# Cross attention and a soft mixture of experts: both halves of a second product planned as one step

## The chip, the cores and the metric

The kernel runs on one core of a Trainium2 chip. The metric is the time of one execution on the device in microseconds (us); the median of several executions is compared. The engines of the core work at the same time, each through its own instructions in the order in which the program lists them: TensorE (PE, with its weight loads PEld) multiplies matrices into PSUM, VectorE (DVE), ScalarE (ACT) and GpSimd (POOL) do elementwise work, and SyncE (SP) starts transfers.

## The reference

Inputs are x (16 batches of 100 tokens, 256 features) and a context (16 x 361 x 256). All numbers are float32.

```python
x = x + xattn(layernorm(x), ctx)          # 16 heads of 16, softmax over 361 keys
z = layernorm(x)
n = layernorm(z) * norm_g + norm_b
logits   = n @ slots_embedded.T           # 100 tokens x 16 experts x 64 slots
dispatch = softmax(logits, axis=tokens)
combine  = softmax(logits, axis=all 1024 slots)
slots = dispatch.T @ n                    # for each expert 64 slots of each batch
h     = gelu(slots @ Wg[e] + bg[e]) * (slots @ Wu[e] + bu[e])   # 256 -> 512
eout  = h @ Wd[e] + bd[e]                 # 512 -> 256
out   = x + combine @ eout
```

Each of the 16 experts has its own three weight matrices of 512 KB; every batch sends 64 slots through every expert.

## The kernel before

The 16 batches go through in five groups, `GROUPS = (2, 2, 4, 4, 4)`. For every group there is attention, then dispatch (logits, softmax over tokens, slots) in quarters of four experts and pairs of batches, then the 16 experts, then the combining of the experts' outputs. The weights of all experts are loaded anew for every group, through six buffers of 512 KB (`load_weights`, `give_back`).

**Products of an expert.** `experts(g)` takes one expert after the other. The first products are made in parts: a PSUM bank `gp` (gate) and a bank `up`, eight matmul instructions each in groups of four batches. ScalarE reads `gp` through gelu into `ge` (L1286), VectorE multiplies with `up` into `hT` (L1291). The second product, `down(g, e, hts)`, takes a pair of experts at once: the first one's 64 slots fill the upper half of the bank's partitions, the second one's the lower half. A bank `dn` holds two batches (2 x 256 columns), so a pair needs one bank in a group of two batches and two banks in a group of four. The loop over `half` makes these banks; each has 32 matmul instructions (L1235) and one VectorE addition of the bias (L1244), which writes `ring`. `down` is called behind the first part of the next pair's first expert (L1304), and once at the end of the group (L1312). After both halves the two experts' `Wd` buffers are given back and refilled.

**Who sets the order.** The program's order is written when the kernel is built, by a planner in the main loop (L1342 to L1465). Every stream of work is a generator. It yields a time from which its next step can run and the number of PSUM banks that it needs; the planner keeps a clock of its own (`Clock`, with planned durations for every engine and a queue of four `mm` banks), and `Task.ready` is the later of that time and of the moment at which the first so many banks of the queue are free (L126, `bank_ready`). At each turn the planner takes the first task in its list that is ready, else the one that is ready soonest, and runs the generator up to its next yield; what lies between two yields stands in the program without a break. The list has attention's units, the dispatch tasks and the side work (keys, queries, output projections) ahead, and the experts last: experts fill whatever the others leave. Once the slots of the next expert are missing, experts aren't ready at all.

**The other streams that matter here.** A unit of attention (`units`, one batch and a quarter of the heads) has three pieces on TensorE: `maxima` (L781) with the `values` (L829) of the unit before, a small transposition in `queries` (L795), and the scores in `exponentials` (L806). Each waits for VectorE or ScalarE behind the one before it. All units share four PSUM banks of their own. `dispatch_quarter` makes logits (`lg`, L938), four exponentials, a reciprocal and a GpSimd product, and then the transposed weights `disp`. From the fourth group on VectorE makes these with 16 transpositions, two for each yield (L1004 to L1011); such a yield needs no bank and waits only until the planner's VectorE is less than 2.5 us behind (L1400 to L1402). Then come two slot products `sl` (L1028), evicted by VectorE and ScalarE. At most two dispatch tasks are in the planner's list at a time.

The four `mm` banks serve `gp`, `up`, `dn`, `cx`, `lg`, `sl`, `po` and the small tiles in turn. On the chip a matmul waits for the bank's last reader by semaphore, whatever the planner assumed.

Of the kernel before, what the change touches and what calls it, by code (L numbers as in the profile page):

```python
# [129 lines left out]
def xattn_ffn_kernel(  # L130
# [38 lines left out]
    def mm_tile(name):  # L169
        return ps_mm.tile([P, 512], F32, tag="mm", name=name)  # L170
# [743 lines left out]
    def eouts_of(g, q):  # L914
        return regions[g, q].rearrange("p (e b d) -> p e b d", e=QE // 2, d=D)
# [301 lines left out]
    def give_back(*names):  # L1217
        for n in names:
            w_free.append(slot_of[n])
            load_weights()  # L1220

    def down(g, e, hts):

        k = g * E + e
        q, j = divmod(e, QE)
        n = GROUPS[g]
        FB = 512 // (n * S)
        for half in range(n // 2):
            yield max(t for h in hts for _, t in h), 1
            dn = mm_tile("dn")  # L1230
            for i in range(2):
                b = 2 * half + i
                for fc in range(FC):
                    for x in range(2):
                        nc.tensor.matmul(  # L1235
                            dn[S * x : S * x + S, i * D : (i + 1) * D],
                            lhsT=hts[x][fc // FB][0].rearrange("p (f b s) -> p f b s", f=FB, s=S)[
                                :, fc % FB, b, :
                            ],
                            rhs=weights[k + x, "wd"][:, fc, :],  # L1240
                            start=fc == 0,
                            stop=fc == FC - 1,
                        )
            nc.vector.tensor_tensor(  # L1244
                eouts_of(g, q)[:, j // 2, 2 * half : 2 * half + 2, :],
                dn.rearrange("p (b d) -> p b d", d=D),
                biases[k // 2].unsqueeze(1).to_broadcast([P, 2, D]),
                ALU.add,
            )
            t = ck.psum_dve(512, ck.pe(2048, ck.bank()))  # L1250
            ck.free(t)
            done_t[g, q] = t
        give_back((k, "wd"), (k + 1, "wd"))

    def experts(g):
        n = GROUPS[g]
        T = n * S
        FB = 512 // T
        pair, to_combine = [], []
        for e in range(E):  # L1260
            k = g * E + e
            q, j = divmod(e, QE)
            hts = []
            for part in range(FC // FB):
                hT = const.tile([P, 512], F32, tag="hT", name="hT", bufs=5)
                ge = two.tile([P, 512], F32, tag="ge", name="ge")
                fcs = range(part * FB, (part + 1) * FB)
                for kind in range(2):
# [33 lines left out]
                if part == 0:  # L1302
                    if e % 2 == 0 and pair:
                        yield from down(g, e - 2, pair)  # L1304
                        pair = []
                    if e % QE == 1 and e > 1:
                        to_combine.append(q - 1)
                    while to_combine and all((g, p) in sums for p in range(n // 2)):
                        yield from combine_quarter(g, to_combine.pop(0))
            give_back((k, "wg"), (k, "wu"))  # L1310
            pair.append(hts)
        yield from down(g, E - 2, pair)  # L1312
        for q in to_combine + [NQ - 1]:
            yield from combine_quarter(g, q)
# [203 lines left out]
```

## Time and profile before

| | us |
|---|---|
| median of 3 runs | 1179.04 (1178.51 to 1179.66) |
| profiled execution | 1181.03 |
| its span, first to last instruction | 1179.2 |
| TensorE busy | 1160.4 |
| VectorE busy | 633.4 |
| ScalarE busy | 540.3 |
| GpSimd busy | 151.4 |
| first gp of the five groups | 84.2, 244.3, 441.6, 775.2, 984.0 |

The mean granted TensorE clock was 0.999. In the second products' row the page has 2048 matmul instructions (L1235), 232.9 us busy in all; every float32 product is two instructions. 512 of them belong to the two groups of two batches together, and 512 to each group of four. TensorE's matmuls overlap, so the duration of one (382 ns) is longer than the time from its start to the next; the time that a run of them holds the engine is read from start to start. The attention of the last group lies within the experts of the third and ends at 783 us; after that the order has experts, dispatch and combining alone.

### The profile page before, as it was taken

What the parts mean: (1) busy time and instruction counts of PE and PEld (TensorE: products, weight loads), DVE (VectorE), ACT (ScalarE), POOL (GpSimd) and SP (SyncE); (2) the same over time, 40 slices, a digit from 0 to 9 for tenths busy, and PEclk for the clock granted to TensorE, in tenths of its full rate; (3) what the DMA queues carried; (4) which work ended last, traced back from release to release, by engine and by line L of the source; (5) the groups of instructions that cost most, each with busy time, mean ns of one, the idle gap of its engine ahead of it and who ended that gap; (6) DMA issues with size and microseconds to landing.
All of it is one profiled execution on the core that took longest, in us unless ns stands there. A gap on an engine that the chain in (4) does not pass through costs nothing.

```text
span 1179.2 us, 24287 instructions
## 1 busy us (share of the span) xinstructions
PE 1160.4 (98%) x9815; PEld 898.6 (76%) x9815; DVE 633.4 (54%) x1559; ACT 540.3 (46%) x1112; POOL 151.4 (13%) x255
## 2 busy tenths in 40 slices
PE   8899999999999999999999999999999999999998
PEld 6588788787788877767777776787878878777876
DVE  5755445566654566655386767656543455432222
ACT  3547553565544667434454634646312336314110
POOL 3110301013000131300010010304000003002000
PEclk9999999999999999999999999999999999999999
DMA  4412666553466603223341321333344343344441
GB/s 133 133 33 83 233 195 202 163 140 120 130 221 224 188 11 90 83 53 106 112 106 54 110 90 39 98 126 112 112 159 138 115 148 126 112 132 159 140 129 55
DMA packets 138578, 144.85 MB, mean 123 GB/s; under 512 B 45040, under 2 KB 97218, under 8 KB 138466
## 3 DMA queue, kind: packets, MB, share of 16 engines
q1 hardware_dynamic: 137358, 141.60, 39.7%
q8 instruction: 78, 1.28, 0.4%
q0 software_dynamic: 496, 1.12, 0.3%
q10 hardware_dynamic: 612, 0.57, 0.2%
q14 instruction: 34, 0.28, 0.1%
HBM read 141.60 MB, written 1.66 MB: 121 GB/s over the span
## 4 chain that ended last, share of the span: by engine, by line
PE 95%; DVE 2%; ACT 2%; issue 1%; DMA 0%; POOL 0%; SPq 0%; ACTq 0%; DVEq 0%; POOLq 0%
PE dn L1235 19%; PE gp L1275 19%; PE up L1275 19%; PE sl L1028 5%; PE po L1157 5%; PE at L806 4%; PE at L781 4%; PE lg L938 3%; PE cx L829 3%; PE k_ps L609 3%; PE v_ps L669 3%; PE o_ps L722 1%; PE at L1329 1%; DVE mxp L786 1%; PE q_ps L538 1%; ACT d_ex L968 1%
## 5 line engine op out<-in xcount | busy, mean ns | idle before, releaser
L1275 PE MATMUL gp<-ring,w_all 128*128 128x256 f32 (+1 forms) x1280 | 247.8, 340 | 1.3 <-ACT lg_all L959 1.3
L1275 PE MATMUL up<-ring,w_all 128*128 128x256 f32 (+1 forms) x1280 | 246.6, 340 | 0.0
L1291 DVE SCALAR_TENSOR_TENSOR hT<-up,parT,ge 128x256 f32<-128x256 f32 (+1 forms) x320 | 119.7, 424 | 233.2 <-PE up L1275 164.3
L1235 PE MATMUL dn<-w_all,hT 128*64 128x256 f32 x2048 | 232.9, 382 | 0.1
L1286 ACT ACTIVATE ge<-gp,parT 128x256 f32<-128x256 f32 (+1 forms) x320 | 117.1, 430 | 249.3 <-PE gp L1275 245.2
L1275 PEld LDWEIGHTS gp<-ring,w_all 128*128 128x128 f32 x1280 | 203.4, 191 | 27.5 <-issue 4.9
L1275 PEld LDWEIGHTS up<-ring,w_all 128*128 128x128 f32 x1280 | 203.7, 191 | 21.4 <-issue 1.2
L1235 PEld LDWEIGHTS dn<-w_all,hT 128*64 128x64 f32 x2048 | 142.7, 137 | 78.5 <-issue 7.8
L786 DVE TENSOR_REDUCE mxp<-at 100x4 f32<-100x1444 f32 x64 | 106.3, 1661 | 30.9 <-PE at L781 30.2
L1244 DVE TENSOR_TENSOR ring<-dn,bd_bc 128x512 f32<-128x512 f32 x64 | 44.3, 692 | 134.8 <-PE dn L1235 133.2
L814 ACT ACTIVATE aT<-at 121x1200 f32<-121x1200 f32 x64 | 75.0, 1171 | 62.9 <-PE at L806 59.5
L1286 ACT ACT_TABLE_LOAD x60 | 77.0, 1283 | 26.7 <-PE gp L1275 26.0
L1008 DVE STREAM_TRANSPOSE disp<-d_ex 32x128 f32<-32x128 f32 x256 | 77.3, 302 | 4.5
L713 POOL TENSOR_TENSOR cxs<-cxs,rs 128x100 f32<-128x100 f32 x63 | 24.9, 398 | 389.3 <-DVE rs L710 361.9
L1043 ACT ACTIVATE ring<-sl,parT 128x256 f32<-128x256 f32 x64 | 32.7, 562 | 67.8 <-PE sl L1028 65.5
L1028 PE MATMUL sl<-disp,xn 100*128 100x256 f32 x256 | 63.4, 388 | 0.2 <-ACT disp L1021 0.2
L1157 PE MATMUL po<-ring,lg_all 128*100 128x256 f32 x256 | 60.5, 383 | 0.4 <-DVE ring L1244 0.2
L993 POOL TENSOR_TENSOR d_ex<-d_ex,d_sm 128x400 f32<-128x400 f32 x28 | 23.9, 854 | 267.6 <-DVE d_sm L990 240.6
L806 PEld LDWEIGHTS at<-q,kT 32*121 32x121 f32 x1344 | 40.6, 180 | 19.9 <-issue 8.8
L1028 PEld LDWEIGHTS sl<-disp,xn 100*128 100x128 f32 x256 | 46.4, 190 | 10.3 <-issue 2.6
L806 PE MATMUL at<-q,kT 32*121 32x100 f32 x1344 | 49.9, 277 | 3.4 <-DVE q L797 3.3
L814 ACT ACT_TABLE_LOAD x36 | 46.2, 1283 | 14.2 <-PE at L806 6.2
(152 smaller groups left out, 1268.8 us busy)
## 6 DMA issues: line engine op xcount, KB each, us to landing
w_all<-in_L_ffn_Wg_dram SPq DMA_DIRECT2D x80, 512.0 KB
w_all<-in_L_ffn_Wu_dram SPq DMA_DIRECT2D x80, 512.0 KB
w_all<-in_L_ffn_Wd_dram SPq DMA_DIRECT2D x80, 512.0 KB
bd_bc<-in_L_ffn_bd_dram SPq DMA_DIRECT2D x80, 64.0 KB
c_sb<-in_ctx_dram SPq DMA_DIRECT2D x96, 44.0 KB
out_dram<-acc SPq DMA_DIRECT2D x8, 200.0 KB
acc<-in_x_dram SPq DMA_DIRECT2D x7, 200.0 KB
ring<-n_L_ffn_slot_embeds_dram POOLq DMA_DIRECT2D x1, 1024.0 KB, 6.8
```

The lines of the kernel that those rows point to most:

```text
L781: nc.tensor.matmul(self.at[:N, r, :S2], lhsT=self.q[rows], rhs=self.k[rows], start=True, stop=True)
L786: nc.vector.tensor_reduce(mxv[:, :, m : m + 1], self.at[:N, :, :S2], AX.X, ALU.max, negate=True)
L806: nc.tensor.matmul(self.at[: KC + 1, r, c * N : (c + 1) * N], lhsT=self.k[rows, c * KC : c * KC + KC + 1], rhs=self.q2[rows], start=True, ...
L814: nc.scalar.activation(self.aT[: KC + 1], self.at[: KC + 1, :, : 3 * N], AF.Exp)
L1008: nc.vector.transpose(dst[toks, :, :, a, :], src[32 * a : 32 * a + 32, :, :, toks])
L1028: nc.tensor.matmul(sl[:, kd * 256 : (kd + 1) * 256], lhsT=xns[g][:, b0 + i, kd * P : (kd + 1) * P], rhs=disp[:, i, :], start=True, stop=True,)
L1157: nc.tensor.matmul(pos[i][:N, :D], lhsT=lg_all[:, slot, 2 * c + i, :], rhs=eouts_of(g, q)[:, c, 2 * p + i, :], start=c == 0, stop=c == 1,)
L1235: nc.tensor.matmul(dn[S * x : S * x + S, i * D : (i + 1) * D], lhsT=hts[x][fc // FB][0].rearrange("p (f b s) -> p f b s", f=FB, s=S)[:, fc ...
L1244: nc.vector.tensor_tensor(eouts_of(g, q)[:, j // 2, 2 * half : 2 * half + 2, :], dn.rearrange("p (b d) -> p b d", d=D), biases[k // 2].uns ...
L1275: nc.tensor.matmul(ps[:, f * T : (f + 1) * T], lhsT=w[:, kd, fc * P : (fc + 1) * P], rhs=slots_of(g, q)[:, j, kd].rearrange("p b s -> p (b ...
L1286: nc.scalar.activation(ge[:, cols], ps[:, cols], AF.Gelu, bias=col(8, e, fc))
L1291: nc.vector.scalar_tensor_tensor(out=hT[:, cols], in0=ps[:, cols], scalar=col(NPAR, e, fc), in1=ge[:, cols], op0=ALU.add, op1=ALU.mult,)
```

## The change

In `down` the yield moves out of the loop over the halves, and asks for as many banks as there are halves: one in groups of two batches, where the loop runs once, and two in groups of four. Both halves' matmuls and bias additions then follow each other in the program without a turn of the planner between them.

```diff
         n = GROUPS[g]
         FB = 512 // (n * S)
+        yield max(t for h in hts for _, t in h), n // 2
         for half in range(n // 2):
-            yield max(t for h in hts for _, t in h), 1
             dn = mm_tile("dn")
             for i in range(2):
                 b = 2 * half + i
```

## The prediction

> **What bounds the kernel now.** I read the page first (busy time, the chain that ended last), then the busy time by stage, then TensorE's waits from the point where the edit can act, and last the order of TensorE's and VectorE's work around single second products.
>
> ```profile
> PE 1160.4 (98%) x9815; PEld 898.6 (76%) x9815; DVE 633.4 (54%) x1559; ACT 540.3 (46%) x1112; POOL 151.4 (13%) x255
> PE 95%; DVE 2%; ACT 2%; issue 1%; DMA 0%; POOL 0%; SPq 0%; ACTq 0%; DVEq 0%; POOLq 0%
> ```
>
> The chain that ended last is 95% TensorE. By stage (columns: length, then busy time and count of PE, PEld, DVE, ACT, POOL, granted clock, DMA share, GB/s):
>
> ```profile
> 393.00:441.00 48.00, 45.66 (x329) 35.02 (x326) 31.03 (x73) 29.54 (x91) 16.21 (x21) 1.00 0.27 63
> 441.00:775.00 334.00, 333.02 (x3097) 244.36 (x3097) 213.04 (x502) 167.57 (x318) 43.44 (x68) 1.00 0.30 87
> 775.00:984.00 209.00, 208.91 (x1270) 166.31 (x1269) 101.95 (x275) 81.89 (x178) 18.60 (x29) 1.00 0.41 127
> 984.00:1180.00 196.00, 190.85 (x1133) 150.19 (x1131) 68.01 (x164) 51.77 (x101) 16.95 (x23) 1.00 0.40 124
> ```
>
> The first four-batch group's experts begin at 441 us, the next two groups' at 775 and 984. The edit can act from the first four-batch second product, at 470 us. TensorE idles 334.00 - 333.02 = 0.98 and 209.00 - 208.91 = 0.09 us in the first two stages; what is missing in the last is the tail after the last product (span end 1179.2). Its waits after 441 us are one:
>
> ```profile
> PE xn_t L748 <- ACT qp L551: 1.0, 1, 1.0
> ```
>
> So no second product waits for a bank. TensorE can end earlier only through 0.98 + 0.09 = 1.07 us of waits or through blocks that themselves become cheaper. That they can is seen in how a second product stands in the order. Split, then whole (start, length, line, tile, count):
>
> ```profile
> 554.86 3.67 PE L1235 MATMUL dn<-w_all,hT 128*64 128x256 f32 x32
> 558.47 0.89 PE L806 MATMUL at<-q,kT 32*121 32x100 f32 x24
> 559.29 3.67 PE L1235 MATMUL dn<-w_all,hT 128*64 128x256 f32 x32
> 562.89 0.87 PE L781 MATMUL at<-kT,qp 32*100 32x361 f32 x8
> ...
> 849.94 7.13 PE L1235 MATMUL dn<-w_all,hT 128*64 128x256 f32 x64
> 857.00 1.35 PE L1275 MATMUL gp<-ring,w_all 128*128 128x256 f32 x5
> ```
>
> A half alone holds TensorE 558.47 - 554.86 = 3.61 and 3.60 us, both halves in one run 857.00 - 849.94 = 7.06 us: 0.15 us less than 7.21.
>
> **The change part by part.** *The yields removed.* Three groups have four batches and eight pairs each, so 24 yields between two halves go. In groups of two batches n // 2 is 1, and nothing differs. Going through all 24 pairs in the trace, TensorE has other work between the halves in 11 (pairs 0 to 3 and 5 to 7 of the first such group, pairs 0 and 7 of the second, 2 and 3 of the last); 13 run whole already. Joining the 11 takes off 11 x 0.148 = 1.63 us, all on the path.
>
> *Where the displaced work goes.* Of the 11 insertions seven are attention's: maxima with values twice (pairs 0, 6), scores twice (2, 5), the small transposition of the maxima twice (1, 7), values with logits once (3). The other four are pieces of dispatch and combining. A displaced piece lands either at a border of gp or up with the joined product, or between gp and up. Start to start, gp and up hold TensorE 1.73 us between their like (785.67 to 787.40), 1.82 before maxima, scores, values or a second product (13 up blocks go straight into a second product, each at 1.82), and 1.83 after them or after a second product. At the border both surcharges are paid already, so the piece costs nothing new; between gp and up it costs 0.09 + 0.10 = 0.20 us. The transposition of the maxima costs 0.02 there, values with logits 0.09, the dispatch pieces nothing (gp beside sl, lg, po stays 1.73). If every displaced attention piece lands between gp and up: 4 x 0.20 + 2 x 0.02 + 0.09 = 0.93 us. Ends: 0, and 11 x 0.20 = 2.2 us. I take 0.93, because borders with second products are two for each pair and are mostly taken.
>
> *Two banks asked for.* The planner now calls the pair ready when the older two of four banks are free in its clock. The second of them belongs to a block at least two mm tiles back in the order, so some 3.5 us old where gp and up came last; only a modelled DVE or ACT queue longer than that delays it. Ends: 0, and one gp or up block (1.73 us) handed to other work in the wrong place now and then, which TensorE doesn't lose, since other work runs. I take 0. On the chip the matmuls still wait for their own banks alone.
>
> *Return of the weights.* give_back comes behind both halves as before; its loads on SP's queue move only with the order. No wait of TensorE on a weight stands in the list after 441 us, with the DMA engines at 0.30 to 0.41. I take 0; the cover is TensorE's own work.
>
> *Steps delayed behind the pair.* What could be planned between the halves now waits up to 3.5 us more. For attention this only exchanges the order of work while experts are there to fill. For dispatch it takes away a place for VectorE's transpositions, also in pairs that TensorE runs whole:
>
> ```profile
> 1027.81 0.88 DVE L1291 SCALAR_TENSOR_TENSOR hT<-up,parT,ge 128x256 f32<-128x256 f32 x2 [2.06 <-PE up L1275]
> 1028.71 0.62 DVE L1008 STREAM_TRANSPOSE disp<-d_ex 32x128 f32<-32x128 f32 x2
> 1031.35 0.69 DVE L1244 TENSOR_TENSOR ring<-dn,bd_bc 128x512 f32<-128x512 f32 x1 [2.02 <-PE dn L1235]
> 1032.07 0.61 DVE L1008 STREAM_TRANSPOSE disp<-d_ex 32x128 f32<-32x128 f32 x2
> 1034.83 0.69 DVE L1244 TENSOR_TENSOR ring<-dn,bd_bc 128x512 f32<-128x512 f32 x1 [2.14 <-PE dn L1235]
> ```
>
> Two transpositions follow each up block (every 3.45 us) and each half; a quarter has 16, so eight such steps. The step at 1032.07, planned between the halves, goes: 3.45 us for each pair that a quarter crosses. What that delays is the dispatch of the last group:
>
> ```profile
> 969.86 1.99 PE L1028 MATMUL sl<-disp,xn 100*128 100x256 f32 x8
> 971.69 1.52 PE L938 MATMUL lg<-xnT,seT 128*128 128x200 f32 x8
> 973.10 1.97 PE L1028 MATMUL sl<-disp,xn 100*128 100x256 f32 x8
> 974.90 1.52 PE L938 MATMUL lg<-xnT,seT 128*128 128x200 f32 x8
> 976.35 3.67 PE L1235 MATMUL dn<-w_all,hT 128*64 128x256 f32 x32
> ...
> 984.01 1.89 PE L1275 MATMUL gp<-ring,w_all 128*128 128x256 f32 x8
> ```
>
> The sl at 969.86 completes the last group's first quarter; its ScalarE eviction ends at 972.91, and the first gp that reads it starts at 984.01, so 11.1 us lie between. The quarter and the one queued before it cross four pairs from 890 to 976: at most 4 x 3.45 = 13.8 us later, some of it won back, because after a joined pair two steps follow within one gp block. Meanwhile TensorE still has the other sl and both lg of these rows to run (1.83 + 1.35 + 1.35 = 4.5 us). Ends: 0 and 13.8 - 11.1 = 2.7 us of waiting. I take 0, as a delay of half the greatest, 6.9 us, stays inside the 11.1.
>
> **Sum.** -1.63 + 0.93 = -0.70 us. The profiled execution took 1181.03 us with a span of 1179.2; the sum would make it 1180.3 and 1178.5. The median of the runs before is 1179.04, 1.99 below that execution, so the forecast is 1178.3.
>
> [...] The rows measure 0.148 for a whole split, so I go by the rows.
>
> **The rivals.** *The last group's experts start late (slower).* Place: the gp at 984.01, and then the one at 1024.08, whose quarter is evicted at 1013.59, 10.5 us ahead. It decides once the dispatch slips by more than 11.1 us; beyond that nothing but dispatch is left, and TensorE idles. Prices: 2.7 us at the first place; the second inherits the slip and crosses one more pair, another 2 to 4 us. With -0.70, +2 to +6: about 1182.5. For it: eight steps in a row that one missed place moves by 3.45 us, and a chain that begins again at once. Against: the 4.5 us of filling, and the two steps after a joined pair. The granted clock stayed 1.00 over the wait of 0.98 us; no wait long enough to show more is in this stage.
>
> *All of the saving and none of the price (faster).* The displaced pieces land on borders (1.63 kept), and the 0.98 us wait at 604 us, where ScalarE's query eviction comes late, is planned away: -1.63 - 1.07 = -2.7 us, 1176.3. For it: the order after 470 us is drawn anew. Against: that wait comes from a burst of VectorE work (keys, transpositions, queries), which a longer gap does not shorten.
>
> *Attention runs behind (slower).* Each joined pair makes one gap of attention 3.45 us longer, at most 16 x 3.45 = 55 us of expert work in two groups, so the middle group's experts could be due before their slots. These first slots were there at 713 us and were used at 775, a margin of 62 us. Price: the stage from 393 to 441 us is such a wait and loses 48.00 - 45.66 = 2.3 us: 1180.6.
>
> *Nothing changes.* Excluded as an order, since 11 pairs do split now; as a time it lies inside the forecast's own range.
>
> **How the numbers follow.** A time within 0.2%, 2.4 us, can't be told from no change here. Forecast, with its neighbours from 1177.0 to 1181.0 (saving 1.63 to price 2.2, and up to 2 us of newly drawn waits): 0.58. Late experts: 0.26, most of it above 1181.4. Faster, below 1176.7: 0.12. Attention behind: 0.04, in part within the bound. That gives 0.12 faster, 0.59 same, 0.29 slower. The range leaves out the lowest tenth and the dearest of the late cases: 1176.8 to 1183.0.
>
> **What would show it.** Right: TensorE's busy time after 441 us falls by 0 to 1.6 us; all 24 second products of these groups are runs of 64, 7.06 us each; the wait list of TensorE stays near 1 us; the pairs of transpositions between the halves are gone. Wrong: a wait at gp on the evictions of sl or on logits near 984 or 1024 us; more blocks of 1.92 us (both surcharges) among gp and up than before; or waits of TensorE on VectorE in the attention stage that sum to over 2 us.

## The result and the profile after

The changed kernel takes 1189.1 us in the median of four runs (1188.24 to 1189.73) against 1179.22 us (1178.51 to 1179.66): a ratio of 1.0079, interval 1.0066 to 1.0092. It is slower by 0.8%, where no change was forecast, and lies outside the range (1176.8 to 1183.0). The profiled execution took 1189.55 us with a span of 1187.7, 8.5 us above the span before.

The page's first and fourth part, after:

```profile
PE 1162.8 (98%) x9815; PEld 901.1 (76%) x9815; DVE 632.4 (53%) x1557; ACT 555.8 (47%) x1126; POOL 150.8 (13%) x255
PE 92%; ACT 3%; DVE 2%; DMA 1%; issue 1%; SPq 0%; POOL 0%; ACTq 0%; DVEq 0%; POOLq 0%
```

The matmuls are as many as before, TensorE is busy 2.4 us longer, and its share of the last chain falls from 95 to 92%. Busy time by stage from the first four-batch expert on (columns: length, then busy time and count of PE, PEld, DVE, ACT, POOL, granted clock, DMA share, GB/s):

```profile
441.00:755.00 314.00, 313.83 (x2788) 232.84 (x2787) 191.34 (x453) 164.52 (x304) 41.81 (x67) 1.00 0.31 92
755.00:965.00 210.00, 209.22 (x1464) 164.52 (x1462) 109.60 (x283) 91.86 (x182) 18.07 (x28) 1.00 0.37 117
965.00:987.00 22.00, 19.76 (x120) 14.89 (x119) 13.21 (x35) 2.90 (x7) 1.04 (x2) 0.92 0.32 111
987.00:1020.00 33.00, 31.89 (x181) 25.84 (x180) 12.07 (x34) 21.41 (x43) 8.81 (x12) 1.00 0.39 124
1020.00:1037.00 17.00, 13.97 (x60) 11.63 (x61) 10.79 (x30) 6.09 (x17) 0.00 (x0) 0.90 0.24 84
1037.00:1188.00 151.00, 146.30 (x896) 113.69 (x890) 45.38 (x103) 30.02 (x60) 8.98 (x12) 1.00 0.37 120
```

Up to 965 us TensorE idles 0.17 + 0.78 us, about as before. What is lost lies in three short stretches between 965 and 1037 us, where the last group's experts begin, and in two of them the granted clock is under 1 (0.92 and 0.90). TensorE's waits after 441 us, longest in total first:

```profile
PE sl L1028 <- DVE disp L1008: 5.3, 2, 3.0
PE gp L1275 <- ACT ge L1286: 1.1, 1, 1.1
PE dn L1235 <- ACT ge L1286: 0.8, 1, 0.8
```

The slot products wait for VectorE's transpositions. The order of TensorE's work at the first of these waits (start, length, line, tile, count, wait before it):

```profile
965.15 7.13 PE L1235 MATMUL dn<-w_all,hT 128*64 128x256 f32 x64
972.21 3.70 PE L1157 MATMUL po<-ring,lg_all 128*100 128x256 f32 x16
978.14 5.41 PE L1028 MATMUL sl<-disp,xn 100*128 100x256 f32 x16 [2.24 <-DVE disp L1008]
983.38 0.38 PE L1075 MATMUL top_t<-ident,top 128*100 128x128 f32 x2
983.61 1.52 PE L938 MATMUL lg<-xnT,seT 128*128 128x200 f32 x8
...
985.30 1.52 PE L938 MATMUL lg<-xnT,seT 128*128 128x200 f32 x8
986.65 1.89 PE L1275 MATMUL gp<-ring,w_all 128*128 128x256 f32 x8
```

In the order before, both sl and both lg ran between the halves of the second product at 966 us. Now the product and the combining (po) are through first, and all that is left waits for the last transpositions. VectorE in the same kernel, around the second product from 947.5 to 954.6 us:

```profile
951.25 0.69 DVE L1244 TENSOR_TENSOR ring<-dn,bd_bc 128x512 f32<-128x512 f32 x1 [2.23 <-PE dn L1235]
954.73 0.69 DVE L1244 TENSOR_TENSOR ring<-dn,bd_bc 128x512 f32<-128x512 f32 x1 [2.79 <-PE dn L1235]
955.34 1.87 DVE L1008 STREAM_TRANSPOSE disp<-d_ex 32x128 f32<-32x128 f32 x6
```

Between the two bias additions VectorE now idles 2.79 us. Before, transpositions stood in the gap of this pair, although TensorE ran its two halves without a break there too (948.64 us, 64 instructions):

```profile
952.97 1.24 DVE L1008 STREAM_TRANSPOSE disp<-d_ex 32x128 f32<-32x128 f32 x4
```

TensorE's second wait is at 1023.43 us, 3.03 us long, ahead of the sl of the second quarter, at the group's fifth expert.

**Where the 8.5 us are.** From 441 us to the last matmul TensorE idles 7.34 us against 1.07: +6.27. Its work, from the first gp at 441 us to the start of the last po and without the waits, is 730.61 us against 728.46: +2.15. Of that the second products give -1.67 (171.05 to 169.38 us, all 24 unbroken at 7.06). The lower clock behind the two waits gives +3.4, as the third experiment shows. The remaining 0.4 us are net of all other blocks, displaced pieces among them.

### The profile page after: what moved, and what is told of

Its sections match the earlier page's. It is cut to its first block, busy times and chain, and to the rows that moved or that the text cites. A ratio compares the mean times of both kernels' runs of the same rounds, so it can differ in the third digit from the quotient of the medians.

```text
span 1187.7 us, 24296 instructions
## 1 busy us (share of the span) xinstructions
PE 1162.8 (98%) x9815; PEld 901.1 (76%) x9815; DVE 632.4 (53%) x1557; ACT 555.8 (47%) x1126; POOL 150.8 (13%) x255
## 3 DMA queue, kind: packets, MB, share of 16 engines
q8 instruction: 78, 1.28, 0.4%
q0 software_dynamic: 496, 1.12, 0.3%
## 4 chain that ended last, share of the span: by engine, by line
PE 92%; ACT 3%; DVE 2%; DMA 1%; issue 1%; SPq 0%; POOL 0%; ACTq 0%; DVEq 0%; POOLq 0%
PE dn L1235 19%; PE gp L1275 18%; PE up L1275 18%; PE sl L1028 5%; PE po L1157 5%; PE at L806 4%; PE at L781 4%; PE lg L938 3%; PE v_ps L669 3%; PE cx L829 3%; PE k_ps L609 3%; PE o_ps L722 1%; ACT d_ex L968 1%; PE at L1329 1%; DVE mxp L786 1%; PE q_ps L538 1%
## 5 line engine op out<-in xcount | busy, mean ns | idle before, releaser
L1235 PE MATMUL dn<-w_all,hT 128*64 128x256 f32 x2048 | 230.5, 381 | 1.1 <-ACT ge L1286 0.8
L1028 PE MATMUL sl<-disp,xn 100*128 100x256 f32 x256 | 66.3, 402 | 5.5 <-DVE disp L1008 5.3
```

The lines of the kernel that those rows point to most:

```text
L1028: nc.tensor.matmul(sl[:, kd * 256 : (kd + 1) * 256], lhsT=xns[g][:, b0 + i, kd * P : (kd + 1) * P], rhs=disp[:, i, :], start=True, stop=True,)
L1235: nc.tensor.matmul(dn[S * x : S * x + S, i * D : (i + 1) * D], lhsT=hts[x][fc // FB][0].rearrange("p (f b s) -> p f b s", f=FB, s=S)[:, fc ...
```

## The experiments

Theory A: the turn of the planner between the halves is one that dispatch's transpositions need, so the last group's slots come late. Rival B: attention, held up by the long pieces, pushes everything behind it. Rival C: the demand for two banks changes the order. The first four kernels were timed side by side, and so were the last four; ratios are to the kernel before.

**1. The last two groups alone.**

```diff
-        yield max(t for h in hts for _, t in h), n // 2
+        joined = g >= 3
+        if joined:
+            yield max(t for h in hts for _, t in h), n // 2
         for half in range(n // 2):
+            if not joined:
+                yield max(t for h in hts for _, t in h), 1
```

> Halves joined in the last two groups alone; the third group, in which attention runs, stays as before. Theory A (a planner's turn between the halves is what dispatch's transpositions need; the last group's slots come late): the waits of TensorE before sl at the last group's first expert and at its fifth are there, 2 to 3 us each with a lower granted clock behind them, and the time is 5 to 10 us above before. Rival B (attention, held up by the long pieces in the third group, pushes everything behind it): within 1 us of before.

1187.8 us, ratio 1.0074 (1.0060 to 1.0088). TensorE's waits after 441 us:

```profile
PE sl L1028 <- DVE disp L1008: 5.3, 2, 3.0
PE gp L1279 <- ACT ge L1290: 1.1, 1, 1.1
PE xn_t L748 <- ACT qp L551: 1.0, 1, 1.0
```

Almost the whole loss is there (0.74 of 0.79%) with attention's order as it was: TensorE's order first differs from that before at 796 us. The three waits are the same to 0.01 us (2.24, 1.12, 3.03). Rival B falls.

**2. The third group alone.** The same edit with `g == 2`.

> Halves joined in the third group alone. Theory A: no wait over 1.1 us behind 441 us, and a time of 0 to 2 us under before (seven splits at 0.15 us go, the displaced pieces of attention cost some of it). Rival B: most of the loss of the changed kernel, 6 to 10 us above before.

1177.7 us, ratio 0.9988 (0.9979 to 0.9996): as theory A expected, and 0.12% faster than before. The waits that are left:

```profile
PE gp L1279 <- ACT ge L1290: 0.5, 1, 0.5
PE k_ps L609 <- DVE cT L595: 0.2, 1, 0.2
```

Here the joined halves do what the first part of the prediction's sum said: TensorE's work from the first four-batch expert on falls from 728.46 to 727.83 us, its waits from 1.07 to 0.65.

**3. The waits filled.** Order as in the changed kernel; only where the planner foresees a wait, small matmuls (L1329) are written instead, 10 and 13 of them (20 and 26 instructions).

```diff
+        if begun and group == len(GROUPS) and waiting and now + 0.3 < ready[first]:
+            warm_up()
+            continue
         task = tasks[first]
```

> The changed kernel with its order as it is, and 10 and 13 small matmuls without use put where the planner foresees TensorE waiting for the last group's slots (behind the po at 972 us and the up at 1021 us). If the lower granted clock behind the two waits costs time of its own: sl and lg behind them hold TensorE 3.5 and 1.7 us instead of 5.2 and 3.0, and the time is 3 to 4 us under the changed kernel, 5 to 7 above before. If the waits alone cost: the time of the changed kernel within 1 us.

1184.09 us, ratio 1.0044 (1.0031 to 1.0056): by the ratios 0.35% or 4.1 us under the changed kernel, at the upper edge of the 3 to 4 expected, and 5.2 above before. TensorE behind the filled waits, then the granted clock in the changed kernel behind the first unfilled one (columns of the latter: stretch in us, length, PE busy, granted clock, DMA share, GB/s):

```profile
977.75 3.72 PE L1028 MATMUL sl<-disp,xn 100*128 100x256 f32 x16
...
984.58 1.89 PE L1275 MATMUL gp<-ring,w_all 128*128 128x256 f32 x8
...
1024.40 1.96 PE L1028 MATMUL sl<-disp,xn 100*128 100x256 f32 x8
...
1027.55 1.89 PE L1275 MATMUL gp<-ring,w_all 128*128 128x256 f32 x8
```

```profile
978.00:979.00 1.00, 0.86 (x4) 1.00 0.55 161
979.00:980.00 1.00, 1.00 (x5) 0.62 0.03 10
980.00:981.00 1.00, 1.00 (x4) 0.50 0.00 0
981.00:982.00 1.00, 1.00 (x4) 0.50 0.00 0
982.00:983.00 1.00, 1.00 (x5) 0.67 0.00 0
```

From sl to gp it takes 984.58 - 977.75 = 6.83 us against 986.65 - 978.14 = 8.51 in the changed kernel, and the second time 3.15 against 1031.31 - 1026.46 = 4.85 us. So 1.68 + 1.70 = 3.4 us of the loss are not the waits but the granted clock of 0.50 behind them, which is 1.00 in this experiment (from 975 to 1000 and from 1020 to 1040 us).

**4. Four transpositions a turn.** In the changed kernel a quarter's dispatch then needs four turns of the planner instead of eight.

```diff
-                        if tb % 2 == 0:
+                        if tb == 0:
                             yield td, 0, (0.0, 0.4, 0.0), "aside"
```

> The changed kernel, with four transpositions for each turn of the planner instead of two, so that a quarter's dispatch needs four turns instead of eight. Theory A: the waits at the last group's first and fifth expert go, and the time is 7 to 11 us under the changed kernel, from 2 us under before to 1 above. Rival B, or a cause in banks or transfers: the time of the changed kernel within 3 us.

1177.37 us, ratio 0.9987 (0.9978 to 0.9996): by the ratios 0.92% or 10.8 us under the changed kernel, and faster than before, with all 24 products unbroken. At the place of the first wait:

```profile
965.83 7.13 PE L1235 MATMUL dn<-w_all,hT 128*64 128x256 f32 x64
972.88 1.99 PE L1028 MATMUL sl<-disp,xn 100*128 100x256 f32 x8
```

The slot product follows the second product without a wait.

**5. A turn for the transpositions alone.** The halves stay joined on TensorE, but the planner gets a turn between them in which only the transposition steps may be picked.

```diff
         yield max(t for h in hts for _, t in h), n // 2
         for half in range(n // 2):
+            if half:
+                middle[0] = True
+                yield max(t for h in hts for _, t in h), 1
+                middle[0] = False
...
+        if middle[0]:
+            tasks = [t for t in tasks if t.aside]
         tasks.append(streams["experts"])
```

> The changed kernel with a turn of the planner between the halves in which it may pick the steps of VectorE's transpositions alone, so that TensorE still has the halves in one run. If the lost turn of the transpositions is the cause: no wait before sl near 976 and 1023 us, 24 unbroken products of 7.06 us, and a time of 1176.5 to 1179, 9 to 12 us under the changed kernel. If the cause is that other TensorE work can't stand between the halves: the time of the changed kernel within 2 us.

1181.07 us, ratio 1.0005 (0.9995 to 1.0015): by the ratios 8.7 us under the changed kernel, level with before. Both expected ranges, 1176.5 to 1179 and 9 to 12 under, were missed a little. At the place of the first wait, and the waits after 441 us:

```profile
965.37 7.13 PE L1240 MATMUL dn<-w_all,hT 128*64 128x256 f32 x64
972.43 1.99 PE L1028 MATMUL sl<-disp,xn 100*128 100x256 f32 x8
```

```profile
PE po L1157 <- ACT lg_all L959: 1.1, 1, 1.1
PE cx L829 <- ACT xnT L754: 0.8, 1, 0.8
PE neg_top L1089 <- ACT ge L1291: 0.8, 1, 0.8
```

Both waits before sl are gone, with every product still unbroken. TensorE's work is 727.55 us, 0.9 under before, but 2.9 us of waits in other places eat that up; they come from the newly drawn order, not from one cause that a run here isolates.

**6. All but the transpositions between the halves.** The kernel before, with its turn between the halves, in which every task but the transposition steps may be picked.

```diff
+            middle[0] = half > 0
             yield max(t for h in hts for _, t in h), 1
+            middle[0] = False
...
+        if middle[0]:
+            tasks = [t for t in tasks if not t.aside]
         tasks.append(streams["experts"])
```

> The kernel before, with its turn of the planner between the halves and all TensorE work allowed there, but no step of the transpositions in that turn. If the lost turn of the transpositions is the cause: the waits before sl come back without any product being joined by the change, and the time is 5 to 10 us above before. If joining on TensorE is the cause: within 1 us of before.

1187.87 us, ratio 1.0069 (1.0051 to 1.0087). Nothing is joined by the edit here (16 of the 24 products run whole, against 13 before), and the loss is there:

```profile
PE sl L1028 <- DVE disp L1008: 5.3, 2, 3.0
PE gp L1278 <- ACT ge L1289: 1.1, 1, 1.1
PE xn_t L748 <- ACT qp L551: 1.0, 1, 1.0
```

The waits at sl and at gp are 2.24, 1.11 and 3.04 us again. With the fifth experiment this settles it: take the transposition steps alone out of the turn, and the loss comes; put them alone back, and it goes.

**7. Four a turn in the kernel before.** The edit of the fourth experiment, without the change.

> The kernel before, with four transpositions for each turn of the planner. It tells what the four alone give: if the time of the joined kernel with four a turn comes from the joined halves, this one stays within 1 us of before; if from the four, it is 1.5 to 3 us under before as well.

1181.54 us, ratio 1.0014 (1.0004 to 1.0025): by the ratio 1.7 us above before, where within 1 us was expected. So four a turn is no gain by itself; TensorE waits 2.67 us in five places, in the attention stage mostly. The fourth kernel is faster than before only with the joined halves too. Both orders are drawn anew, and how much of the difference between the two is the luck of that is not shown.

**8. Two banks for each half.** `yield ..., 1` becomes `yield ..., n // 2` in the loop before; the halves stay two steps.

> The kernel before, halves as two steps, each of them asking for two banks. Both theories: within 1 us of before, as no wait on a bank is in the trace. If asking for two banks is a cause: 2 us or more above before.

1180.1 us, ratio 0.9996 (0.9987 to 1.0005). TensorE's order is that of the kernel before row for row; VectorE's differs in one place. Rival C falls.

## Why the prediction was wrong

**What bounds the kernel** was right: TensorE without waits in the four-batch stages, no bank waited for.

**The saving** was right: forecast 1.63 us from 11 joined products, measured 1.67 (171.05 to 169.38).

**The displaced pieces**, forecast +0.93, are not more than that: in the second experiment the joined third group lowers TensorE's work by 0.63 us net, and in the fifth, with all three groups joined, by 0.91. The two parts together were forecast at -0.70.

**Two banks** at 0 and **the return of the weights** at 0 were right: the eighth experiment has the first alone, and no wait on a weight appears. One second product of the changed kernel, at 841.77 us, does wait 0.78 us for ScalarE's gelu reads; the wait of 0.98 us that the kernel before had is gone in exchange.

**The step that failed** is "Steps delayed behind the pair", and in it the sentence "I take 0, as a delay of half the greatest, 6.9 us, stays inside the 11.1". The mechanism was named and priced there, and the lost step of each pair was right. Two sizes were wrong: the margin and the delay. The margin of 11.1 us ran from 972.91 to the gp at 984.01. TensorE's rows before, at the start of that second product and at the end of the margin:

```profile
966.25 3.67 PE L1235 MATMUL dn<-w_all,hT 128*64 128x256 f32 x32
...
979.96 0.42 PE L1075 MATMUL top_t<-ident,top 128*100 128x128 f32 x2
980.22 1.89 PE L1157 MATMUL po<-ring,lg_all 128*100 128x256 f32 x8
981.94 0.51 PE L1089 MATMUL neg_top<-dg,ones 100*128 100x200 f32 x2
982.28 1.89 PE L1157 MATMUL po<-ring,lg_all 128*100 128x256 f32 x8
```

Start to start, the second half (3.61 us) and the two po (3.45) are 7.06 us of work that needs nothing late. The other 4.04 us are the end of a lg, then sl, lg, top_t and neg_top, which are dispatch themselves or follow it. Counting them as "filling" was the error: the second sl waits for the same row of VectorE steps, and new logits start only once a quarter in the planner's list is done. So TensorE had 7.1 us of cover, not 11.1.

The delay was more than half the greatest, too. The first sl started 969.86 - 966.25 = 3.61 us behind the start of the second product before, and 978.14 - 965.15 = 12.99 us behind it in the changed kernel, a slip of 9.38 us. TensorE ran out of other work at 975.90, which covered 975.90 - 965.15 - 3.61 = 7.14 of them; 2.24 remain, which is the wait. By the forecast's own subtraction neither error makes a wait alone: 6.9 us would have stayed inside 7.1, and 9.4 inside 11.1. The slip was within the forecast's bound of 13.8; why it was 9.4 and not less, no run takes apart.

**The rival "The last group's experts start late"** is what happened, at both places named, with a chance of 0.26; TensorE waits there at the sl, one step ahead of the gp that was named. The price of that case, +2 to +6 us with the -0.70 in it, was too small against the 8.5 us of the spans because of two things. The lower clock behind the waits was left at nothing (3.4 us). And a third wait of 1.11 us follows at 997 us, where a gp waits for its bank until ScalarE has read the gelu input. ScalarE in the changed kernel ahead of it:

```profile
990.23 1.28 ACT L1286 ACT_TABLE_LOAD   x1
991.53 0.84 ACT L1286 ACTIVATE ge<-gp,parT 128x256 f32<-128x256 f32 x2
992.38 1.28 ACT L1126 ACT_TABLE_LOAD   x1
...
996.10 1.28 ACT L1286 ACT_TABLE_LOAD   x1
997.40 1.57 ACT L1286 ACTIVATE ge<-gp,parT 128x256 f32<-128x256 f32 x4
```

The late quarters bring their exponentials among the gelus, and a table load of 1.28 us stands at each change. This third wait stands wherever the dispatch is late (experiments 1, 3 and 6) and is gone at this place where it is not (2, 4 and 5); no run took it away alone.

**The rivals "Attention runs behind"** (first experiment: almost the same loss without joined halves in attention's stage; second: none with them there alone) and "All of the saving and none of the price" did not happen. The second came nearly true where the loss can't arise: joined in the third group alone, 0.12% faster.

**The chances** followed from the wrong margin: with 7.1 us of cover in place of 11.1, half of the greatest delay, 6.9 us, already reaches nearly to its edge, and by that reckoning the late start would have been about as likely as not.

## What to carry to other kernels

A step boundary in a planned order is a resource of every engine's queue, not only of the one whose work is being merged. Before taking one away, list who was served there: here VectorE's 0.6 us steps that TensorE's rows don't show at all, eight in a row with one for each boundary. And a margin up to a deadline counts only with work that can run if the late thing is late; what depends on it is no cover.

## What the runs showed of the hardware

Short waits of TensorE cost more than their length in some places here, and in others not. Behind the wait of 2.24 us the granted clock was 0.50 from 979.24 to 982.65 us in the changed kernel, while it stayed at 1.00 behind the same wait in the first and sixth experiments (both sl in 3.72 us there, 5.41 here). Behind the wait of 3.03 us (3.04 in the sixth experiment) it fell to 0.50 in all three, for 3.41 us in the changed kernel, for 3.4 us in the first experiment (0.66 in the mean of 1024 to 1029 us) and for 6.8 us in the sixth. Filled with small matmuls, neither wait cost any clock (1.00 from 975 to 1000 and from 1020 to 1040 us). Two of these stretches, from the changed kernel and from the sixth experiment:

```profile
979.25:982.64 3.39, 3.39 (x10) 0.50 0.00 0
1023.50:1030.30 6.80, 6.79 (x18) 0.50 0.08 31
```

The length of a wait alone does not sort these cases. In the changed kernel the clock was 0.50 in three stretches before 1187 us, each 3.41 us long: from 43.99, from 979.24 and from 1027.03 us. The moments 982.65, 1027.03 and 1030.44 come 1, 14 and 15 times 3.413 us after 979.24. The first stretch, before any expert runs, came behind waits of 0.35 and 0.88 us; behind the waits of 0.78 us, which ends at 841.77, and of 1.11 us, which ends at 998.29, the clock stayed at 1.00. What decides whether the clock falls behind a wait, no run here shows. Why it stayed low twice as long in the sixth experiment is open as well.
